# Polynomial convolution and self-attention on one core: the second image of the first pair in double chunks, and a new order in the first image's prologue

## The chip, the cores and the metric

One core of a Trainium2 chip runs the whole problem in one launch. The metric is the device time of that launch in microseconds; lower is better. Engines are named as in the profile: PE (matrix), PEld (its weight load), DVE (vector), ACT (scalar), POOL (GpSimd), SP (the queue that starts most transfers).

## The reference, cut to what matters

The input is 32 images of 64 channels and 56 x 56 pixels, in fp32. Layer 0 is a polynomial in each group of 8 channels, added to the input. Layer 1 is a non-local block whose attention matrix is normalised twice.

```python
# layer 0, per image, groups of 8 channels
p2 = x[:, :, I2] * x[:, :, J2]                  # all 36 pairs of a group
y2 = einsum(p2, W2) + b2
p3 = x[:, :, I3] * x[:, :, J3] * x[:, :, K3]    # all 120 triples
y3 = einsum(p3, W3) + b3
l  = inp + y2 * beta2 + y3 * beta3 * 0.1

# layer 1, per image, n = 56*56 = 3136 positions
g     = clip(bn1(conv1x1(l, w_inside)), 0, 6)
theta = l[:, :32]
f     = theta^T theta                           # 3136 x 3136
f     = softmax(f, over rows); f = softmax(f, over columns)
out   = f g / h * w
out   = bn2(depthwise3x3(out, w_dw)) + l
```

## The kernel before

Images go in 16 pairs, one image on each half of the 128 partitions. A pair is 49 attention tiles of 128 positions (24 for each image, and one that holds both remainders); `IT = 49`. For each tile `t` the loop issues `scores` in two halves (PE into PSUM, then DVE takes minima and copies out), `first_softmax` and `second_softmax` (two exponentials of 128 x 3136 on ACT), and, `LAG = 3` tiles later, `attend` (100 matmul records of PE into the `av` and `ax` banks). Between these, in gaps called `aux0` and `aux1`, stand *units* of other work: polynomial matmuls of an image to come (`poly`), or the 1x1 convolution (`g_in`). Both use the one PSUM region `ax`, so units follow each other: a unit fills it, `poly_out` or `g_out` takes it out on DVE, `prepare` sets it up again.

The polynomial of an image is worked in chunks of 242 columns (`PCH`, 13 chunks, the last of 232). For each chunk, SP loads rotated copies of the input ("0", "a", "2", "4", "b", and two of an unrotated copy, "c", held in `xc`); the generator `products` multiplies them on POOL: `q = x0*xa`, four rounds `q*x`, and one product of the two `xc`. `poly` multiplies each round by its weights. For later pairs all four 32-row groups `ks` of a pair are worked at once (`ALL`). In pair 0 the first image is made in a prologue, and the second (`TWO`, groups 2 and 3) during the first 14 tiles; then pair 1's 13 chunks (`ALL`) follow in the remaining tiles of pair 0.

Loads are limited by slots: `XB` gives 7 for "0" copies, 13 for other copies, 3 for `xc`; `ROOM` gives 8 for `q` and 20 for products. `plan` is the order of the loads, `prefetch` issues from it while slots and `credit` allow, `advance` issues products while `ROOM` allows. `held` and `taken` count at issue; the engines then wait on semaphores.

The prologue works the first image in 7 columns of 448 (`FCS`). `first_loads` issues 16 transfers, half on SP and half on ACT, into 28 parts of four tiles; `first_products` makes 11 products on DVE, `first_poly` multiplies them on PE, `first_out` adds the bias and the input, `first_g` makes the 1x1 convolution of the positions that are complete. Batch norm's constants need a square root on ACT. Theta of the first image is copied by `load_theta` through SP in two parts.

Every engine's instructions are kept in the order of the code (`Pinned`), by a helper whose line is 108. So all rows of the profile say L108, and tiles tell them apart.

```python
for c in range(1, NF):
    first_poly(c)
    first_out(c - 1)
    if c + 2 < NF:
        first_loads(c + 2)
    if c + 1 < NF:
        first_products(c + 1)
    if c == 5:
        load_theta(0, 0, FCS[5][0])
        for b in range(NPC):
            feed(0, b, TWO)
        credit[0] = 12
        advance()
    first_g(c - 1)
```

Of the kernel before, what the change touches and what calls it, by code (L numbers as in the profile page):

```python
# [35 lines left out]
PCH = -(-N // NPC)  # L36
PCS = [(p, min(PCH, N - p)) for p in range(0, N, PCH)]
NROT = 6
EXT = CPG + NROT - 1
# [30 lines left out]
def tile_poly_conv_attention(  # L70
# [136 lines left out]
    fx, fp = parts(firsts), parts(ys[1:] + [tt])  # L207
    fat = {"x": 0, "p": 0, "q": 0}
    fxs = {}
# [74 lines left out]

    s1 = rsqrt_eps("bn1", row("var1"), C)
    dve.tensor_tensor(s1, s1, row("gamma1"), ALU.mult)
    for j in range(2):
        dve.tensor_tensor(wit[:, j, :], wit[:, j, :], s1, ALU.mult)
    bias1 = const.tile([128, C], FP, name="bias1")
    dve.tensor_tensor(bias1, row("mean1"), s1, ALU.mult)  # L290
    dve.tensor_tensor(bias1, row("beta1"), bias1, ALU.subtract)
    bias1r = const.tile([128, GM, C], FP, name="bias1r")
    for k in range(GM):
        dve.tensor_copy(bias1r[:, k, :], bias1)


    s2 = rsqrt_eps("bn2", col("var2"), 1)
    dve.tensor_tensor(s2, s2, col("gamma2"), ALU.mult)
    dve.tensor_scalar(wdt, wdt, s2, W / H, ALU.mult, ALU.mult)
    bias2 = const.tile([128, 1], FP, name="bias2")  # L300
    dve.tensor_tensor(bias2, col("mean2"), s2, ALU.mult)
    dve.tensor_tensor(bias2, col("beta2"), bias2, ALU.subtract)

    prods = {}
# [9 lines left out]

    XB = {"x0": 7, "xs": 13, "xc": 3}
    held = dict.fromkeys(XB, 0)
# [4 lines left out]

    def start(out, in_):
        credit[0] -= 1
        sync.dma_start(out=out, in_=in_)

    def load_next():
        tag, key = plan.pop(0)  # L330
        n, c, ks, name, k = key
        p0, w = PCS[c]
        held[tag] += 1
        ident = f"{n}_{c}_{ks[0]}_{k}"
        if name == "c":
            t = xp.tile([128, 2, PCH], FP, name=f"xc_{ident}", tag=tag, bufs=XB[tag])
            at = slice(ks[0] * 32, ks[-1] * 32 + 32)
            for d in range(2):
                src = bass.AP(
                    x.tensor,  # L340
                    ((4 * n + ks[0]) * EXT + 4 * d) * 4 * N + p0,
                    [[EXT * 4 * N, len(ks)], [N, 32], [1, w]],
                )
                start(t[at, d, :w], src)
            loaded[key] = [t[at, d, :w] for d in range(2)]
            return
        t = xp.tile([128, PCH], FP, name=f"x{name}_{ident}", tag=tag, bufs=XB[tag])
        for s0, every, d, grow in LOADS[name]:
            src = bass.AP(
                x.tensor,  # L350
                ((4 * n + k) * EXT + d) * 4 * N + p0,
                [[N, 32], [grow * 4 * N, NSLOT // every], [1, w]],
            )
            start(t[s0::every, :w] if every > 1 else t[:, :w], src)
        loaded[key] = t[:, :w]

    def prefetch():
        while plan and held[plan[0][0]] < XB[plan[0][0]] and credit[0] >= 1:
            load_next()


    ROOM = {"q": 8, "pr": 20}
    taken = dict.fromkeys(ROOM, 0)

    def products(n, c, ks):

        p0, w = PCS[c]  # L370
        ident = f"{n}_{c}_{ks[0]}"

        def use(name, k=None):
            key = n, c, ks, name, k
            return loaded.pop(key)

        x0 = {}
        rounds = [{}]
        both = []
        prods[n, c, ks] = rounds, both  # L380
        yield "q", len(ks)
        for k in ks:
            yield "load", (n, c, ks, "a", k)
            x0[k] = use("0", k)
            xa = use("a", k)
            q = prp.tile([128, PCH], FP, name=f"q_{ident}_{k}", tag="q", bufs=ROOM["q"])[:, :w]
            pool.tensor_tensor(q, x0[k], xa, ALU.mult)
            rounds[0][k] = q
            held["xs"] -= 1
            prefetch()  # L390
        for r, of in enumerate(("0", "2", "4", "b")):
            rounds.append({})
            yield "pr", len(ks)
            for k in ks:
                if of != "0":
                    yield "load", (n, c, ks, of, k)
                xr = x0[k] if of == "0" else use(of, k)
                p = prp.tile([128, PCH], FP, name=f"p_{ident}_{k}_{r}", tag="pr", bufs=ROOM["pr"])[:, :w]
                pool.tensor_tensor(p, rounds[0][k], xr, ALU.mult)
                rounds[-1][k] = p  # L400
                held["x0" if of == "0" else "xs"] -= 1
                prefetch()
        at = slice(ks[0] * 32, ks[-1] * 32 + 32)
        yield "load", (n, c, ks, "c", None)
        yield "pr", 1
        both += use("c")
        p4 = prp.tile([128, PCH], FP, name=f"p4_{ident}", tag="pr", bufs=ROOM["pr"])[at, :w]
        pool.tensor_tensor(p4, both[0], both[1], ALU.mult)
        rounds.append({k: p4 for k in ks})
# [26 lines left out]
    def feed(n, c, ks):  # L436
        todo = [("x0" if name == "0" else "xs", name, k) for k in ks for name in "0a"]
        for name in "24bc":
            todo += [("xc", name, None)] if name == "c" else [("xs", name, k) for k in ks]
        for tag, name, k in todo:  # L440
            plan.append((tag, (n, c, ks, name, k)))
        feeds.append((products(n, c, ks), None))
# [11 lines left out]

    def poly(n, c, ks, rs):

        p0, w = PCS[c]
        rounds = prods[n, c, ks][0]
        at = slice(ks[0] * 32, ks[-1] * 32 + 32)
        for r in rs:  # L460
            for k in ks:
                pe.matmul(
                    out=ax[k * 32 : k * 32 + 32, AUX : AUX + w],
                    lhsT=wq[:, r, k % 2, :] if r < NRND else w4[at, k * 32 : k * 32 + 32],
                    rhs=rounds[r][k],
                    start=False,
                    stop=(r == NRND),
                    skip_group_check=True,
                )
            taken["pr" if r else "q"] -= 1 if r == NRND else len(ks)  # L470

    def poly_out(n, c, ks):

        p0, w = PCS[c]
        at = slice(ks[0] * 32, ks[-1] * 32 + 32)
        assert n < 3 or all((n - 3, b) in stored for b in range(NB))
        xc = prods.pop((n, c, ks))[1][0]
        held["xc"] -= 1
        dve.scalar_tensor_tensor(
            ys[n % 3][at, p0 : p0 + w], ax[at, AUX : AUX + w], bias0[at], xc, ALU.add, ALU.add  # L480
        )
# [3 lines left out]

    def load_theta(b, c0=0, c1=N):
        y = ys[b // 2 % 3]
# [3 lines left out]
        for r in range(4):  # L491
            start(ths[b][r * 32 : r * 32 + 32, c0:c1], y[p0 : p0 + CRED, c0:c1])

# [187 lines left out]
    def make_diags():  # L681

        eye = xp.tile([128, PCH], FP, name="eye", tag="xs", bufs=XB["xs"])[:, :128]
        pool.memset(eye, 0.0)
# [4 lines left out]
        for k in range(9):  # L689
            t = xp.tile([128, PCH], FP, name=f"diag_{k}", tag="xs", bufs=XB["xs"])[:, :128]  # L690
            pool.tensor_scalar(t, eye, wdt[:, k : k + 1], None, ALU.mult)
            diags.append(t)
# [47 lines left out]
    LAG = 3  # L740
    ALL, ONE, TWO = (0, 1, 2, 3), (0, 1), (2, 3)
    last = NP * IT
# [30 lines left out]

    def poly_unit(n, c, ks, rs, hs):
        ends = rs[-1] == NRND
        unit(
            hs,
            FOR_POLY,
            lambda: poly(n, c, ks, rs),
            (lambda: poly_out(n, c, ks)) if ends else None,  # L780
            1 + 3.6 * len(rs),
        )
        if ends and c == NPC - 1:
            for j in (0, 1):
# [38 lines left out]

    def first_g(c):
        for qs in GS:
            if min(len(FCS) - 1, ((qs[-1] + 1) * QT - 1) // FW) == c:
                g_in(0, qs, 0)
                g_out(0, qs, 0)
                prepare(FOR_G if qs[0] < NQ else FOR_POLY)

    prepare(FOR_G)
    NF = len(FCS)
    first_poly(0)
    for c in range(1, NF):
        first_poly(c)
        first_out(c - 1)
        if c + 2 < NF:
            first_loads(c + 2)
        if c + 1 < NF:
            first_products(c + 1)  # L840
        if c == 5:
            load_theta(0, 0, FCS[5][0])

            for b in range(NPC):
                feed(0, b, TWO)
            credit[0] = 12
            advance()
        first_g(c - 1)
    first_out(NF - 1)
    load_theta(0, FCS[5][0], N)  # L850
    first_g(NF - 1)


# [4 lines left out]
    for n in range(NP):  # L858
# [4 lines left out]
        def rounds(m, c, ks, per):  # L863
            return [("p", m, c, ks, list(range(r, r + per))) for r in range(0, NRND + 1, per)]

        todo = []
        if n == 0:
            for c in range(NPC):
                todo += rounds(0, c, TWO, 3)
# [196 lines left out]
```

## Time and profile before

| | |
|---|---|
| three runs | 4947.52, 4949.45 and 4963.6 us; median 4949.45 |
| the profiled execution | 4948.12 us, of which the span is 4946.3 us |
| granted PE clock, mean | 0.992 |
| first exponential (tile 0) starts | 97.09 us |
| stretch 97 to 218 us: PE busy | 105.13 of 121.00 us |
| stretch 218 to 503 us: PE busy | 256.25 of 285.00 us |
| stretch 503 to 797 us (one later pair): PE busy | 288.38 of 294.00 us |

A row of the time order gives start and duration in microseconds, engine, operation, output and inputs by the program's names, shape and count; in brackets stand the idle time of the engine before it and what ended that. A row of a table of stretches gives its length, the busy time of PE, PEld, DVE, ACT and POOL with the counts, the granted PE clock, and the share and rate of DMA. In rows of groups the busy time and the mean duration in ns are followed by the idle time before the group and its releasers. PE records each matmul of this kernel twice.

### The profile page before, as it was taken

The numbers are of one execution on the slowest core, as the hardware profiler recorded it, in microseconds if no ns is written. First come the engines' busy times: TensorE is split into PE (matmuls) and PEld (weight loads), VectorE is DVE, ScalarE is ACT, GpSimd is POOL, SyncE is SP. The second block draws the span as 40 slices with busy tenths as digits, with TensorE's granted clock in tenths as the row PEclk, the third lists the DMA queues.
The fourth block names the chain that finished last, engine by engine and source line by source line (L and its number), as shares of the span: only waits on it lengthen the run. The fifth ranks groups of instructions, "written<-read, shape, count | busy, mean of one in ns | idle before, by whom it ended". The sixth has DMA issues, their size and how long they took to land.

```text
span 4946.3 us, 264020 instructions
## 1 busy us (share of the span) xinstructions
PE 4734.2 (96%) x118122; PEld 3218.8 (65%) x118122; DVE 4125.5 (83%) x6100; ACT 4554.4 (92%) x2356; POOL 3222.6 (65%) x4335
## 2 busy tenths in 40 slices
PE   6898999999999999999999999999999999999887
PEld 2555666666666666666666666666666666666665
DVE  6545898888888898888889889898888889888887
ACT  1667999999999999999999999999999999999996
POOL 2677685858858586785857768585875858678000
PEclk8999999999999999999999999999999999999999
DMA  7555656565565655556555565656556565654201
GB/s 205 145 152 156 147 144 153 144 152 141 145 141 151 146 145 149 143 143 146 149 143 144 149 143 142 154 144 150 142 145 143 150 144 144 153 142 126 45 11 34
DMA packets 884318, 685.66 MB, mean 139 GB/s; under 512 B 290924, under 2 KB 869356, under 8 KB 879084
## 3 DMA queue, kind: packets, MB, share of 16 engines
q1 hardware_dynamic: 875180, 659.46, 52.5%
q8 instruction: 924, 15.14, 1.3%
q10 hardware_dynamic: 8000, 9.30, 0.6%
q14 instruction: 214, 1.75, 0.1%
HBM read 565.65 MB, written 25.69 MB: 120 GB/s over the span
## 4 chain that ended last, share of the span: by engine, by line
PE 77%; DVE 12%; DMA 3%; issue 3%; ACT 3%; POOL 1%; SPq 1%; ACTq 0%; DVEq 0%; POOLq 0%
PE av L108 33%; PE ps L108 26%; PE ax L108 18%; DVE e L108 10%; ACT e L108 3%; DMA xc_None<-in_x_dram 1%; POOL p L108 1%; DVE y L108 1%; DMA first<-in_x_dram 1%; DVE num L108 1%; DMA x<-in_x_dram 1%; SPq L108 1%; DMA xa<-in_x_dram 0%; DVE rd L108 0%; ACTq L108 0%
## 5 line engine op out<-in xcount | busy, mean ns | idle before, releaser
L108 PEld LDWEIGHTS av<-gq,e 128*64 128x64 f32 x64512 | 2012.2, 138 | 943.9 <-issue 936.2
L108 ACT ACTIVATE e<-e,nm 128x3136 f32<-128x3136 f32 x784 | 2283.6, 2913 | 279.9 <-DVE e L108 264.0
L108 POOL TENSOR_TENSOR p<-q,x 128x242 f32<-128x242 f32 (+1 forms) x2418 | 1824.3, 788 | 815.6 <-PE ax L108 801.2
L108 ACT ACTIVATE e<-e,rz 128x3136 f32<-128x3136 f32 x784 | 2270.3, 2896 | 0.0
L108 PE MATMUL av<-gq,e 128*64 128x65 f32 x64512 | 2225.5, 225 | 3.9 <-ACT e L108 3.1
L108 DVE TENSOR_SCALAR_CACHE_REDUCE e<-ps 128x1568 f32<-128x1568 f32 x784 | 1403.7, 1790 | 314.1 <-PE ps L108 294.2
L108 DVE TENSOR_SCALAR_CACHE_REDUCE e<-ps,nm 128x1568 f32<-128x1568 f32 x784 | 1448.6, 1848 | 255.7 <-PE ps L108 250.1
L108 PE MATMUL ps<-th 32*64 32x392 f32 x25088 | 1449.4, 515 | 120.7 <-DVE e L108 110.7
L108 POOL TENSOR_TENSOR q<-x,xa 128x242 f32<-128x242 f32 x806 | 574.2, 734 | 226.0 <-DMA xa<-in_x_dram 218.0
L108 DVE SCALAR_TENSOR_TENSOR y<-tt,wdt,y 128x605 f32<-128x605 f32 (+6 forms) x711 | 713.1, 1003 | 6.4 <-DMA tt<-tr 5.2
L108 POOL TENSOR_TENSOR p<-q,xb 128x242 f32<-128x242 f32 x806 | 573.9, 739 | 212.3 <-PE ax L108 204.5
L108 PEld LDWEIGHTS ps<-th 32*64 32x64 f32 x25088 | 369.8, 130 | 463.7 <-DVE e L108 381.5
L108 PE MATMUL ax<-gq,e 128*64 128x65 f32 x12288 | 489.7, 222 | 0.7 <-issue 0.6
L108 PE MATMUL ax<-p,wq 128*32 128x242 f32 (+1 forms) x6448 | 481.9, 374 | 1.8 <-POOL p L108 0.2
L108 PEld LDWEIGHTS ax<-gq,e 128*64 128x64 f32 x12288 | 425.0, 138 | 1.0 <-issue 1.0
L108 PEld LDWEIGHTS ax<-p,wq 128*32 128x32 f32 x6448 | 178.4, 109 | 111.8 <-POOL p L108 19.1
L108 POOL TENSOR_SCALAR y<-y,bias 128x616 f32<-128x616 f32 (+2 forms) x79 | 146.9, 1860 | 98.9 <-PE ax L108 98.9
L108 POOL TENSOR_TENSOR p<-xc_None 128x242 f32<-128x242 f32 (+3 forms) x208 | 127.6, 614 | 109.5 <-DMA xc_None<-in_x_dram 91.0
L108 DVE SCALAR_TENSOR_TENSOR y<-ax,bias,xc_None 128x242 f32<-128x242 f32 (+3 forms) x208 | 97.1, 467 | 116.8 <-PE ax L108 116.8
L108 PE MATMUL ax<-wit,y 128*64 128x64 f32 x3136 | 144.2, 223 | 11.7 <-issue 7.5
L108 PE MATMUL ax<-p,w 128*32 128x242 f32 (+1 forms) x1612 | 123.9, 370 | 32.1 <-POOL p L108 32.1
L108 ACT ACTIVATION_READ_ACCUMULATOR e<-e,nm 128x1 f32 x784 | 145.5, 186 | 0.0
(86 smaller groups left out, 1389.4 us busy)
## 6 DMA issues: line engine op xcount, KB each, us to landing
x<-in_x_dram SPq DMA_DIRECT2D x2232, 121.0 KB
xa<-in_x_dram SPq DMA_DIRECT2D x744, 121.0 KB
xb<-in_x_dram SPq DMA_DIRECT2D x1488, 60.5 KB
th<-y SPq DMA_DIRECT2D x124, 392.0 KB
xc_None<-in_x_dram SPq DMA_DIRECT2D x360, 121.0 KB
x<-in_x_dram SPq DMA_DIRECT2D x186, 116.0 KB
out_dram<-y SPq DMA_DIRECT2D x60, 308.0 KB
tt<-tr SPq DMA_DIRECT2D x128, 100.0 KB
```

The source lines that it names most:

```text
L108: i = f(*args, **kw)
```

## The change

In pair 0 the second image is worked in double chunks of 484 columns: one load, and one POOL product, covers two chunks, and PE multiplies the two halves one after the other, in the units and the order of before. The two `xc` copies still come by single chunks. Slots become parts of one ring tile for each kind, and a double takes two neighbouring ones. `XB` goes from 7, 13 and 3 to 6, 14 and 3.

In the prologue, a column's way out and the first G matmuls of the column before it go ahead of its polynomial on PE; what remains of G follows one column later. Batch norm's constants move into the loop, behind `first_loads(3)`. The feed of the second image starts at column 4 rather than 5, and both parts of theta are copied through ACT.

```diff
+DCS = [(p, min(2 * PCH, N - p)) for p in range(0, N, 2 * PCH)]
...
-    s1 = rsqrt_eps("bn1", row("var1"), C)
...
-    XB = {"x0": 7, "xs": 13, "xc": 3}
+    XB = {"x0": 6, "xs": 14, "xc": 3}
...
+    ring = {t: [xp.tile([128, m, PCH], FP, name=f"ring_{t}", tag=t, bufs=1), 0] for t, m in XB.items() if t != "xc"}
+    ringc = xp.tile([128, 2 * XB["xc"] * PCH], FP, name="ring_xc", tag="xc", bufs=1)
+
+    def chunks(ks):
+        return DCS if len(ks) < len(ALL) else PCS
+
+    def many(w):
+        return -(-w // PCH)
+
+    def take_ring(tag, w):
+        t, at = ring[tag]
+        m, size = many(w), t.shape[1]
+        if at % m or at + m > size:
+            at = 0
+        ring[tag][1] = (at + m) % size
+        return t[:, at : at + m, :].rearrange("p m w -> p (m w)")[:, :w]
...
-            q = prp.tile([128, PCH], FP, name=f"q_{ident}_{k}", tag="q", bufs=ROOM["q"])[:, :w]
+            q = take_ring("q", w)
             pool.tensor_tensor(q, x0[k], xa, ALU.mult)
...
-        p4 = prp.tile([128, PCH], FP, name=f"p4_{ident}", tag="pr", bufs=ROOM["pr"])[at, :w]
-        pool.tensor_tensor(p4, both[0], both[1], ALU.mult)
+        p4 = take_ring("pr", w)[at, :]
+        for sub in range(m):
+            yield "load", (n, c, ks, f"c{sub}", None)
+            both.append(use(f"c{sub}"))
+            pool.tensor_tensor(p4[:, sub * PCH : min((sub + 1) * PCH, w)], *both[sub], ALU.mult)
...
-            taken["pr" if r else "q"] -= 1 if r == NRND else len(ks)
+            if ends:
+                taken["pr" if r else "q"] -= (sub + 1) * (1 if r == NRND else len(ks))
...
+    def first_units(c):
+        return [qs for qs in GS if min(len(FCS) - 1, ((qs[-1] + 1) * QT - 1) // FW) == c]
+
+    def first_g(c, at=0):
+
+        for i, qs in enumerate(first_units(c)):
+            if at != 1 or i:
                 g_in(0, qs, 0)
+            if at is not None:
                 g_out(0, qs, 0)
                 prepare(FOR_G if qs[0] < NQ else FOR_POLY)
+            else:
+                return
...
     for c in range(1, NF):
-        first_poly(c)
         first_out(c - 1)
+        if c > 1:
+            first_g(c - 2, 1)
         if c + 2 < NF:
             first_loads(c + 2)
+        if c == 1:
+
+            s1 = rsqrt_eps("bn1", row("var1"), C)
...
+            prepare(FOR_G)
+        first_g(c - 1, None)
+        first_poly(c)
         if c + 1 < NF:
             first_products(c + 1)
+        if c == 4:
+
+            for b in range(len(DCS)):
+                feed(0, b, TWO)
+        if c >= 4:
+            credit[0] = 8
+            advance()
         if c == 5:
-            load_theta(0, 0, FCS[5][0])
-
-            for b in range(NPC):
-                feed(0, b, TWO)
-            credit[0] = 12
-            advance()
-        first_g(c - 1)
+            load_theta(0, 0, FCS[5][0], act)
     first_out(NF - 1)
-    load_theta(0, FCS[5][0], N)
+    load_theta(0, FCS[5][0], N, act)
+    first_g(NF - 2, 1)
     first_g(NF - 1)
```

## The prediction

> **What bounds the kernel now.** I read the page's engine and slice lines first, then stretches of the span, then the time order inside the two stretches that the change touches, then the chain and POOL's groups there.
>
> ```profile
> PE 4734.2 (96%) x118122; PEld 3218.8 (65%) x118122; DVE 4125.5 (83%) x6100; ACT 4554.4 (92%) x2356; POOL 3222.6 (65%) x4335
> 97.00:218.00 121.00, 105.13 (x1944) 60.03 (x1946) 62.09 (x98) 78.69 (x42) 91.15 (x138) 0.97 0.55 145
> 218.00:503.00 285.00, 256.25 (x5564) 160.05 (x5558) 157.26 (x248) 202.88 (x105) 197.13 (x297) 0.95 0.58 152
> 503.00:797.00 294.00, 288.38 (x7396) 198.91 (x7400) 256.88 (x376) 284.57 (x148) 211.90 (x278) 1.00 0.59 148
> ```
>
> The three stretches (PE, PEld, DVE, ACT, POOL busy, then clock and DMA) are: second image of pair 0 (97 to 218), all of pair 1's polynomial (218 to 503), and one later pair. A later pair takes 294 us with PE at 98%, and the same holds for every pair behind it. Pair 0 takes 406 us. In 97 to 218 PE is busy 105 of 121 us and nobody else is full: something is late.
>
> ```profile
> 116.78 2.91 ACT L108 ACTIVATE e<-e,nm 128x3136 f32<-128x3136 f32 x1 [0.88 <-DVE e L108]
> 217.75 2.91 ACT L108 ACTIVATE e<-e,nm 128x3136 f32<-128x3136 f32 x1 [3.98 <-DVE e L108]
> 161.83 0.60 PE L108 MATMUL ax<-q,wq 128*32 128x242 f32 x4
> 169.55 0.60 PE L108 MATMUL ax<-q,wq 128*32 128x242 f32 x4
> 181.60 1.01 PE L108 MATMUL ax<-p,wq 128*32 128x242 f32 x8
> 184.40 0.60 PE L108 MATMUL ax<-p,w 64*32 64x242 f32 x4 [1.79 <-POOL p L108]
> ...
> by line: DMA x<-in_x_dram 34.0%; POOL p L108 26.6%; SPq L108 17.3%; DMA xc_None<-in_x_dram 9.9%; issue 8.9%; DMA xb<-in_x_dram 7.0%; DVE e L108 4.0%; POOLq L108 0.2%
> 121.15 4.47 DMA xc_None<-in_x_dram
> ...
> L108 POOL TENSOR_TENSOR p<-q,x 128x242 f32<-128x242 f32 x67 | 44.8, 708 | 0.0
> L108 POOL TENSOR_TENSOR p<-xc_None 64x242 f32<-64x242 f32 x12 | 7.3, 612 | 28.8 <-DMA xc_None<-in_x_dram 25.3 <-PE ax L108 2.3 <-PE ps L108 1.2
> ```
>
> From tile 3 (116.78) to tile 14 (217.75) a tile takes 9.18 us. A tile in which PE waits for nobody takes 7.72 (161.83 to 169.55, same first unit a tile later); the usual one stalls before the last matmuls of a chunk (181.60 to 184.40). The chain of 120 to 165 is a loop of SP issues, transfers and POOL products, with no PE in it. POOL sits idle 28.8 us before the product of the two xc copies, because xc stands last in SP's order. SP gives 14 transfers per chunk at about 0.6 us each, 8.4 us plus waits for slots, and a chunk takes 9.3.
>
> The prologue is the other stretch:
>
> ```profile
> 34.02 1.28 ACT L108 ACT_TABLE_LOAD   x1 [34.02 <-DMA first<-in_x_dram]
> 35.61 0.55 DVE L108 RECIPROCAL r_bn<-s_bn 128x64 f32<-128x64 f32 x1 [4.88 <-ACT s_bn L108]
> 41.40 0.60 DVE L108 TENSOR_TENSOR tt<-first 128x448 f32<-128x448 f32 x1
> 79.97 0.61 DVE L108 TENSOR_TENSOR first<-first 64x448 f32<-64x448 f32 x1
> 87.47 1.61 PE L108 MATMUL ps<-th 32*64 32x392 f32 x16
> 91.04 4.10 PE L108 MATMUL ps<-th 32*64 32x392 f32 x16 [1.96 <-DVE e L108]
> 97.09 2.91 ACT L108 ACTIVATE e<-e,nm 128x3136 f32<-128x3136 f32 x1 [23.95 <-DVE e L108]
> ```
>
> DVE stands still until ACT has issued column 2's loads and can take the square root of the batch norm; products of column 2 start at 41.40, column 6's end at 80.58, the first exponential starts at 97.09, after a wait for theta's tail in the matmuls of 91.04.
>
> **The change part by part.**
>
> *Double chunks.* Per two chunks SP issues 16 transfers instead of 28 (xc stays in single chunks): 9.6 us. POOL does 10 products of 484 columns and two of xc. The trace has no 484-wide product. Upper bound twice the row, 2 x 708 = 1416 ns; below, 232 wide takes 682 to 688 and 242 wide 708, some 2.3 ns a column, so about 1250. The Trainium skill's "GPSIMD Engine Reference" (Performance versus the Vector engine) gives 2.6 cycles an element[...]. I take 1250, nearest to the trace. The sum is 10 x 1.25 + 2 x 0.61 = 13.7 us ([...]by the upper bound 15.4); PE needs two tiles, 15.4. So the verdict, PE bound, is the same with each.
>
> The slots decide whether it gets there. A double chunk takes 18 of the 20 pr slots, and they come free only as its second half is multiplied. With T the start of a chunk's third PE unit, POOL can do all but one product of the next chunk's first round from T+1.0: four products to T+6, three more (free since unit four, T+4.4) to T+9.8, then xc to T+11. PE wants the first three rounds at T+7.7 and xc's product at T+12.5. The margin is 1.5 us, 0.5 with the upper bound. The next chunk's q and first product end at T+14.8, before T+15.4.
>
> Here a rule speaks against the change: "DMA: Bandwidth & Descriptors" (Rules for kernel authors) says that a DMA whose outermost dimension has size c below 16 runs on at most c engines. The xc loads of this phase have 2 outermost, and stay so. The row agrees: 4.47 us to land for 60.5 KB, beside 3.13 for an x of 121 KB soon after. If the four in a row serialized into POOL's path as the two do now, the 28.8 us of idle would stay and the gain would be near nothing. I take the gain: the loads go out 10 us ahead of their product once SP is not full.
>
> Worth: tiles 3 to 14 take 11 x 7.72 less 1.35 for the one unit that its tile 8 lacks (0.43 + 0.92), 83.6 instead of 101.0: minus 17.4. The half clock at the end of the stretch (mean 0.97) may give 1 more; I leave 1.5 for small stalls. **Minus 17.**
>
> *Prologue order.* Removed: PE's first G matmuls behind a whole column of polynomial. Moved: batch norm behind first_loads(3). By the order of the changed program's instructions ACT now issues eight more loads before its square root, and every PE matmul of column 1 stands behind G of column 0, which needs batch norm. ACT's 8 loads took 6 us in before (38.75 to 44.80); now they start at 34.5, each behind the landing of the transfer eight places earlier, so the table load is near 42, and products of column 2 at 42 + 6.8 = 48.8 (6.8: 34.02 to 41.40 less the column's way out, now earlier). PE then starts column 1 after an idle stretch of 20 us. In before the clock is 0.50 from about 37 to 47 after an idle of 7; "TensorE: Matmul & The Clock Gate" (The HAM clock gate) says that an idle window of 3.4 us halves the clock until about as long of work: at full clock column 1 costs nothing beside DVE, at half clock its 4.8 us become about 7, and DVE's way out waits 2 us. By the row I take 2.
>
> Then DVE: 5.97 of products, 0.60 way out, 0.75 for G's way out and refill, 7.3 a column with no PE wait (before 7.1 to 9.3). End of products: 48.8 + 2 + 4 x 7.3 + 6 = 86.0 (was 80.58). Tail: way out, refill and first G 1.9; column 6's matmuls, now behind them, 4.8 (29.22 to 34.05); way out 0.7; three G rounds at 1.43, 4.3; two score halves with DVE 1.72 + 1.85 + 1.72 + 1.9. Together 18.8 (was 16.5). First exponential 104.8: **plus 8**, bounds plus 3 (ACT's loads at pure issue rate, warm clock) and plus 13.
>
> *Theta on ACT.* SP's queue loses 8 issues, theta's tail no longer stands behind 12 copies: minus 2.5, already in the tail above. But transfers take turns on eight semaphores, and theta's last one now follows a copy that waits for the ninth product of the first double chunk. POOL starts that near 85, the ninth ends at 96, its copy lands at 99, theta at 101.5, and the exponential follows 3 us later: 104.5, level with the other path, so not added. DMA queue order is what is queued behind it: SP's next copies, with time to spare.
>
> *Early feed.* Doubles go out from column 4: no cost ahead of the last first loads in SP's order; a chunk ready by 99, wanted at 106.
>
> *Rings, 6 and 14 slots.* From the first scores on, PE and DVE have the same instructions. In later pairs POOL waits 801 us for PE in one group of the page alone, which covers it; zero, bound plus 0.5 a pair either way.
>
> Sum against the profiled execution (4948.1 us; span 4946.3; 1.3 below the runs' median of 4949.45): 4948.1 - 17 + 8 = 4939.
>
> **The rivals.** (1) The prologue costs 0 to 2, as the matmuls of a column no longer tie DVE and loads(3) start 8 us earlier; against it stands DVE waiting on ACT; 4931. (2) The slots or the narrow xc loads stall each double chunk 2 us and more, or theta's semaphore adds 8: gain and loss cancel; for it the thin margin; 4950. (3) Slower: x0 falls from 7 to 6 slots in all pairs, SP stands before an x0 slot with theta, tt and out behind it, and PE waits at pair ends. Price: 15 pairs; from 1.6 us a pair (24 in all) it decides over my minus 9; at 1.8 a pair 4966. Against it: SP has some 370 transfers a pair (13 x 26, and theta, tt and out) at 0.64, about 235 of 294 us. (4) Doubles that do not arise: the instruction order shows them, so no chance.
>
> **How the numbers follow.** 0.3% (15 us) is about what a measurement can tell from no change. Likeliest 0.64, 4939; rival 1 0.17, 4931; rival 2 0.12, 4950; rival 3 0.07, 4966. Faster by over 0.3%, below 4933: most of rival 1 and a tenth of the likeliest, 0.21; slower, over 4963: rival 3 and a part of 2, 0.09; same 0.70. Range: plus 3 with minus 19, and rival 1, reach 4926; rival 2 reaches 4953.
>
> **What would show it.** After: tiles 3 to 14 at 7.7 to 7.9 us, POOL's wait for xc near nothing, 484-wide products near 1250 ns, table load near 42, first exponential near 105, the pair-1 stretch and later pairs unchanged. Wrong if tiles stay over 8.5, if the first exponential is before 99 or after 112, or if a later pair is off 294 by over 1.

## The result and the profile after

| | before | changed |
|---|---|---|
| median, 12 runs each (us) | 4951.25 | 4952.55 |
| span of the profiled execution (us) | 4946.3 | 4946.9 |
| first exponential starts (us) | 97.09 | 124.44 |
| mean tile from tile 3 to tile 14 (us) | 9.18 | 7.56 |
| first POOL product of pair 1 (us) | 213.7 | 217.1 |
| tile 48, the last of pair 0 (us) | 488.3 | 490.6 |

The ratio is 0.9997, 95% interval 0.9988 to 1.0005: no difference that can be measured. Two large changes cancel. The second image gained what was forecast, and the prologue lost more than three times what was forecast. (The kernel before was run again beside each experiment below, with medians from 4948.70 to 4948.96 us; ratios are to those runs.)

First the engines' line of the changed kernel's profile and its three stretches (PE, PEld, DVE, ACT, POOL busy, then clock, DMA share, GB/s):

```profile
PE 4722.0 (95%) x118122; PEld 3215.6 (65%) x118122; DVE 4120.5 (83%) x6100; ACT 4553.9 (92%) x2356; POOL 3208.4 (65%) x4275
97.00:218.00 121.00, 103.70 (x1812) 55.48 (x1810) 62.25 (x99) 73.75 (x39) 81.13 (x81) 0.89 0.54 151
218.00:503.00 285.00, 259.05 (x5696) 164.51 (x5696) 162.07 (x256) 209.11 (x109) 198.86 (x300) 0.94 0.58 151
503.00:797.00 294.00, 288.62 (x7394) 199.03 (x7378) 256.89 (x374) 281.57 (x147) 212.50 (x278) 1.00 0.58 146
```

The first stretch hides both changes: PE is busy for 103.70 us where it was 105.13, because 27 us of it are now prologue (its clock of 0.89 says so too), and the rest runs faster. The second stretch holds more PE work, 259.05 us against 256.25, which the prediction did not have. The later pair is as it was.

The second image, by tiles 3 and 14 in the time order, and then by POOL's groups between 97 and 218 us:

```profile
144.22 2.91 ACT L110 ACTIVATE e<-e,nm 128x3136 f32<-128x3136 f32 x1 [0.88 <-DVE e L110]
227.37 2.91 ACT L110 ACTIVATE e<-e,nm 128x3136 f32<-128x3136 f32 x1 [1.47 <-DVE e L110]
```

```profile
L110 POOL TENSOR_TENSOR ring_pr<-ring_q,ring_xs 128x484 f32<-128x484 f32 x36 | 42.6, 1227 | 0.0
L110 POOL TENSOR_TENSOR ring_pr<-ring_q,ring_x 128x484 f32<-128x484 f32 x10 | 12.2, 1223 | 29.5 <-PE ax L110 29.5
L110 POOL TENSOR_TENSOR ring_pr<-ring_xc 64x242 f32<-64x242 f32 x12 | 7.2, 616 | 6.8 <-DMA ring_xc<-in_x_dram 4.9 <-issue 1.5
```

Eleven tiles take 83.15 us instead of 100.97. A product of 484 columns takes 1227 ns. POOL waits 4.9 us for the xc copies; in the kernel before it was 27.4 in this stretch (total, number of waits, longest):

```profile
POOL p L108 <- DMA xc_None<-in_x_dram: 27.4, 11, 4.9
```

What POOL waits for now is PE, which has to free slots: 29.5 us, of which one wait of 18.6 is PE's late start.

The prologue, by the same rows that the prediction showed of before:

```profile
42.99 1.28 ACT L110 ACT_TABLE_LOAD   x1 [42.99 <-DMA first<-in_x_dram]
44.57 0.55 DVE L110 RECIPROCAL r_bn<-s_bn 128x64 f32<-128x64 f32 x1 [11.66 <-ACT s_bn L110]
49.78 0.61 DVE L110 TENSOR_TENSOR tt<-first 128x448 f32<-128x448 f32 x1
83.54 0.62 DVE L110 TENSOR_TENSOR tt<-first 128x448 f32<-128x448 f32 x1 [3.06 <-DMA first<-in_x_dram]
88.37 0.61 DVE L110 TENSOR_TENSOR first<-first 64x448 f32<-64x448 f32 x1
97.36 0.68 DVE L110 SCALAR_TENSOR_TENSOR y<-first,bias,first 64x448 f32<-64x448 f32 x1 [7.12 <-PE first L110]
101.86 2.86 PE L110 MATMUL ps<-th 32*64 32x392 f32 x12
109.89 1.57 PE L110 MATMUL ps<-th 32*64 32x392 f32 x4 [5.17 <-DMA th<-y]
120.93 1.57 PE L110 MATMUL ps<-th 32*64 32x392 f32 x4 [1.09 <-DMA th<-y]
124.44 2.91 ACT L110 ACTIVATE e<-e,nm 128x3136 f32<-128x3136 f32 x1 [5.46 <-DVE e L110]
```

Batch norm's wait grew from 4.88 to 11.66 us, as forecast. Scores begin at 101.86 (87.47 before), and then tile 0 takes 22.6 us to its exponential where it took 9.6. Of the time from 101.86 to 120.93, PE spends most in front of theta. The chain of waits of this stretch says what theta stood behind (start, duration, what):

```profile
94.20 4.79 POOL ring_pr L110 x5
...
100.00 1.18 POOL ring_pr L110
101.17 10.37 DMA ring_xs<-in_x_dram
...
111.61 5.47 DMA ring_xs<-in_x_dram
117.07 0.02 issue
117.09 3.79 DMA th<-y
120.88 0.04 issue
120.93 1.59 PE ps L110 x4
```

A POOL product, the eighth, frees the slot of a prefetch copy; that copy takes 10.37 us to land; the next copy on its completion semaphore (the counter that says that a transfer has landed) is issued at its landing; theta's last transfer is on that semaphore too, and is issued on ACT at 117.09, right behind the second landing.

### The profile page after: what moved, and what is told of

Same layout as the page of the kernel before. It is cut to its first block, busy times and chain, and to the rows that moved or that the text cites. A ratio compares the mean times of both kernels' runs of the same rounds, so it can differ in the third digit from the quotient of the medians.

```text
span 4946.9 us, 263995 instructions
## 1 busy us (share of the span) xinstructions
PE 4722.0 (95%) x118122; PEld 3215.6 (65%) x118122; DVE 4120.5 (83%) x6100; ACT 4553.9 (92%) x2356; POOL 3208.4 (65%) x4275
## 4 chain that ended last, share of the span: by engine, by line
PE 78%; DVE 11%; issue 3%; DMA 3%; ACT 3%; POOL 1%; SPq 1%; ACTq 0%; DVEq 0%; POOLq 0%
PE av L110 33%; PE ps L110 26%; PE ax L110 19%; DVE e L110 9%; ACT e L110 3%; DMA ring_xs<-in_x_dram 2%; POOL ring_pr L110 1%; DVE y L110 1%; DVE num L110 1%; SPq L110 1%; DMA ring_xc<-in_x_dram 1%; DMA first<-in_x_dram 1%; PE first_s L110 0%; DMA th<-y 0%; POOL ring_q L110 0%
## 5 line engine op out<-in xcount | busy, mean ns | idle before, releaser
L110 POOL TENSOR_TENSOR ring_pr<-ring_q,ring_xs 128x242 f32<-128x242 f32 (+2 forms) x2382 | 1784.5, 783 | 533.7 <-PE ax L110 522.8
L110 POOL TENSOR_TENSOR ring_pr<-ring_q,ring_x 128x242 f32<-128x242 f32 (+2 forms) x794 | 606.2, 789 | 607.4 <-PE ax L110 574.8
L110 POOL TENSOR_TENSOR ring_q<-ring_x,ring_xs 128x242 f32<-128x242 f32 (+2 forms) x794 | 570.3, 745 | 169.3 <-DMA ring_xs<-in_x_dram 166.4
L110 PE MATMUL ax<-ring_pr,wq 128*32 128x242 f32 (+1 forms) x6448 | 474.5, 373 | 2.2 <-POOL ring_pr L110 1.1
L110 PEld LDWEIGHTS ax<-ring_pr,wq 128*32 128x32 f32 x6448 | 177.0, 109 | 106.9 <-POOL ring_pr L110 13.3
L110 DVE SCALAR_TENSOR_TENSOR y<-ax,bias,ring_xc 128x242 f32<-128x242 f32 (+3 forms) x208 | 97.0, 467 | 102.6 <-PE ax L110 102.6
L110 POOL TENSOR_TENSOR ring_pr<-ring_xc 128x242 f32<-128x242 f32 (+3 forms) x208 | 127.7, 615 | 67.8 <-DMA ring_xc<-in_x_dram 59.2
L110 PEld LDWEIGHTS ax<-wit,y 128*64 128x64 f32 x3136 | 118.9, 139 | 37.0 <-issue 18.7
## 6 DMA issues: line engine op xcount, KB each, us to landing
ring_xs<-in_x_dram SPq DMA_DIRECT2D x1440, 60.5 KB
```

What stands on the lines that cost most here:

```text
L110: i = f(*args, **kw)
```

## The experiments

*Theory A*: theta on ACT takes its turn on the DMA semaphores between prefetch copies that wait for POOL, and this, not the doubles or the load on the engines, holds tile 0. *Rival*: the transfer engines are full, and theta is late in any order. *Theory B*: the gain of the second image comes from the double chunks. *Rival*: from the slots and rings, or from the lead that a late PE gives POOL. A third question came up on the way: why pair 1 ended only 2.3 us later than before when tile 15 was 8.7 us late.

**theta_sp: the changed kernel, theta on SP, and the prefetch around it held to 8 and then 4 issues.**

```diff
-        if c >= 4:
-            credit[0] = 8
-            advance()
+            credit[0] = 8
+            advance()
         if c == 5:
-            load_theta(0, 0, FCS[5][0], act)
+            load_theta(0, 0, FCS[5][0])
+            credit[0] = 4
+            advance()
     first_out(NF - 1)
-    load_theta(0, FCS[5][0], N, act)
+    load_theta(0, FCS[5][0], N)
```

The first two added lines stand under `if c == 4:`.

> The changed kernel with theta's eight transfers on SP: head ahead of the third round's copies, tail behind the last column's way out and ahead of the xc copies. Main theory: what held tile 0 from 101.9 to 120.9 us was theta on ACT, each transfer behind a prefetch copy on the same DMA semaphore. Then theta's tail lands near 102, the first exponential is at 109 (101.9 plus the 7.3 us of four score groups with DVE between them) instead of 124.4, tiles 3 to 13 stay at 7.72, and the time falls by about 15 us, to 4937. Rival: the transfers are slow because the engines are full with prefetch copies in any order; then theta lands after 108, the first exponential is at 115 to 119, and the time falls by 5 to 9.

Measured: 4935.09 us, ratio to before 0.9976 (0.9967 to 0.9985). The first exponential is at 111.87; the scores start at 103.77, two microseconds late because the table load was (45.11), and take 8.1 us to the exponential. In the time order:

```profile
93.36 4.24 SPq L110 DMA_DIRECT2D th<-y  x4
101.61 3.66 SPq L110 DMA_DIRECT2D th<-y  x4
103.77 2.59 PE L110 MATMUL ps<-th 32*64 32x392 f32 x16
105.31 2.38 SPq L110 DMA_DIRECT2D ring_xc<-in_x_dram  x4
111.87 2.91 ACT L110 ACTIVATE e<-e,nm 128x3136 f32<-128x3136 f32 x1 [23.29 <-DVE e L110]
```

Theta's last transfer is issued by 105 and lands at 107.5, later than the 102 expected and near the rival's 108, yet PE hardly waits for it now (0.7 us at its weight loads). 12.6 us of the late start are gone, and 17 us of the time by the medians (10 by the two ratios to before). The edit moves the prefetch copies too, so the next run changes the queue alone.

**old_theta_act: the converse, one edit.** The double chunks behind the old prologue (old_prologue, below), and theta on ACT.

```diff
-            load_theta(0, 0, FCS[5][0])
+            load_theta(0, 0, FCS[5][0], act)
...
-    load_theta(0, FCS[5][0], N)
+    load_theta(0, FCS[5][0], N, act)
```

> As old_prologue, with one edit: theta's eight transfers on ACT instead of SP. In program order they then take the semaphores that they have in the changed kernel, the last one behind the copy that waits for POOL's ninth double product. Main theory: this alone brings the late start. POOL's products begin 4.7 us earlier here than in the changed kernel (84.9 against 89.6), where theta's last transfer landed at 120.9; so it lands near 116, the first exponential is near 119 to 120 instead of 96.5, and the time rises from 4925.7 to 4945 to 4950. Rival: theta was late only because the changed kernel's prologue gave the copies out too early and too many; then the first exponential is at 97 to 104 and the time stays under 4933.

Measured: 4941.31 us, ratio to before 0.9976 (0.9964 to 0.9988), against 4925.66 for old_prologue. The first exponential is at 114.49 instead of 96.53, 18 us later, where 23 were expected and the rival had at most 7: theta landed at 110.9. Its chain of waits has the same links as the changed kernel's, a copy of 9.22 us and one of 5.23 on theta's semaphore:

```profile
91.73 0.91 POOL ring_pr L110
92.65 9.22 DMA ring_xs<-in_x_dram
...
101.94 5.23 DMA ring_xs<-in_x_dram
107.17 0.02 issue
107.19 3.74 DMA th<-y
110.93 0.04 issue
110.97 1.59 PE ps L110 x4
```

So the choice of queue for eight transfers costs, by itself, 18 us at the first exponential, and 16 us of the whole time by the medians (9 by the ratios, whose intervals overlap a little). In the instructions of all these runs the transfers of SP and ACT share eight completion semaphores, and each waits for the landing of the one before it on its own. On SP, theta's place among the copies is fixed by SP's order; on ACT it is fixed by nothing but the turn that it was given.

**bn_back: theta_sp, and batch norm where it was.**

```diff
     first_loads(2)
+    s1 = rsqrt_eps("bn1", row("var1"), C)
...
-        if c == 1:
-            s1 = rsqrt_eps("bn1", row("var1"), C)
...
```

> As theta_sp, and the batch norm back ahead of the loop (before column 3's loads on ACT). Main theory: table load near 34 instead of 43, DVE's wait for the square root near 5 instead of 11.7, column 2's products start near 42, and all of it reaches the end of the prologue: first exponential near 101, time about 4929. Rival: column 6's loads, 3 us late in the changed kernel, become the bound and give half of it back: 105, 4933.

Measured: 4925.86 us, ratio 0.9956 (0.9941 to 0.9971). The first exponential is at 102.27, 9.6 us earlier than in theta_sp:

```profile
33.31 1.28 ACT L110 ACT_TABLE_LOAD   x1 [33.31 <-DMA first<-in_x_dram]
34.90 0.55 DVE L110 RECIPROCAL r_bn<-s_bn 128x64 f32<-128x64 f32 x1 [4.20 <-ACT s_bn L110]
```

The main theory holds, with the first exponential 1.3 us behind its 101 and the time 3 us under its 4929; column 6's loads were late by 3.0 us here as in the changed kernel, and cost nothing more.

**old_prologue: doubles and rings, all of the old prologue.** Theta on SP, batch norm ahead of the loop, the old order of a column, feed at column 5.

```diff
-        first_out(c - 1)
-        if c > 1:
-            first_g(c - 2, 1)
...
-        first_g(c - 1, None)
         first_poly(c)
+        first_out(c - 1)
...
+        first_g(c - 1)
...
```

> Double chunks, rings and slots of the changed kernel, with the prologue of the kernel before in its order, theta on SP. Main theory: first exponential at 97 to 100, tiles 3 to 13 at 7.72, so tile 15 is 16 to 19 us earlier than in the kernel before; pair 1's stretch is a chain of loads and products whose end moves with its start, which takes another 6; time about 4927. Rival: the second image was only fast because the late start gave POOL a lead of 27 us; then tiles 3 to 13 average over 8.2 and the time is 4936 or more.

Measured: 4925.66 us, ratio 0.9957 (0.9942 to 0.9971); first exponential at 96.53, tiles 3 to 14 at 7.56 us, tile 15 19.0 us earlier than before, tile 48 25.3 us. Each number is within 1.5 us of the main theory's. With POOL 11.7 us ahead of the first exponential, as in the kernel before (11.8), and not 34.8 as in the changed one, the doubles are as fast. Against bn_back it starts 5.7 us earlier and ends level. Taken out one after the other, theta's queue, batch norm's place and the rest of the new prologue give back 12.6, 9.6 and 5.7 us at the first exponential.

**single: the changed kernel, single chunks.**

```diff
-DCS = [(p, min(2 * PCH, N - p)) for p in range(0, N, 2 * PCH)]
+DCS = PCS
```

> The changed kernel with single chunks for the second image too (rings, slots 6 and 14 and the new prologue stay). Main theory: the double chunks alone bring the gain of the second image, so tiles 3 to 13 are back near 9.2 us; the copies ahead of theta's tail are half as large and wait for fewer products, so the first exponential is at 112 to 120; the end of pair 1 comes later by as much as the first image's second half does; time about 4966. Rival: the new slot counts or the rings bring the gain; then tiles 3 to 13 stay near 7.7 and the time is near 4945.

Measured: 4960.57 us, ratio 1.0019 (1.0009 to 1.0029). Slower, as the main theory had it, but tiles 3 to 14 are at 7.80 us, which is the rival's number and not the 9.2 of the main theory. The first exponential is at 121.28, and POOL had begun at 88.0: 33 us of lead instead of 12. So either the slots or the lead makes up for the single chunks.

**single_old: the same edit on old_prologue.**

> The prologue of the kernel before and single chunks, only the rings and the slot counts 6 and 14 of the change left. Main theory: rings and slots do nothing, so tiles 3 to 13 are back at 9.2 us, POOL's products for the second image take 125 to 130 us (127.7 in the kernel before), pair 1's begin near 213, and the time is that of the kernel before within 4 us. Rival: the slots, not the doubles, shortened the second image; then tiles 3 to 13 are at 7.8 and the time is near 4930.

Measured: 4948.09 us, ratio 0.9997 (0.9988 to 1.0006); tiles 3 to 14 at 9.10 us, POOL's second image 128.4 us long. Rings and slots do nothing that can be measured. In single it was the lead: the same slow chain, started 33 us ahead of PE, is only caught up at the end, where tile 13 takes 9.73 us.

That answers theory B and leads to the third question. From the time order of POOL, in nine kernels:

| kernel | POOL, second image: first to last product | POOL, pair 1 | tile 15, against before | pair 1's first product, against before | tile 48, against before |
|---|---|---|---|---|---|
| before | 85.3 to 213.0 | 213.7 to 462.7 | 0 | 0 | 0 |
| changed | 89.6 to 216.4 | 217.1 to 464.0 | +8.7 | +3.4 | +2.3 |
| single | 88.0 to 222.7 | 223.4 to 472.7 | +9.8 | +9.7 | +10.0 |
| single_old | 84.9 to 213.4 | 214.0 to 464.4 | +0.4 | +0.4 | +3.0 |
| theta_sp | 91.8 to 203.7 | 204.4 to 453.0 | -4.0 | -9.3 | -9.7 |
| old_theta_act | 82.6 to 206.1 | 206.8 to 453.7 | -1.5 | -6.9 | -8.1 |
| bn_back | 80.9 to 194.2 | 194.8 to 440.1 | -13.5 | -18.8 | -22.6 |
| xc_early | 87.1 to 195.0 | 195.7 to 444.5 | -12.7 | -18.0 | -19.4 |
| old_prologue | 84.9 to 188.7 | 189.3 to 437.4 | -19.0 | -24.3 | -25.3 |

Pair 1's products take 245 to 250 us in each kernel, and tile 48 follows the start of the last one by 24 to 27 us. The changed kernel and single reach tile 15 within 1.1 us of each other and end pair 0 7.7 us apart; POOL's starts on pair 1 are 6.3 apart.

The two marks are not free of each other. With double chunks the first product of pair 1 stands 16.4 us ahead of tile 15, in all seven such kernels (early_bn, below, is the seventh); with single chunks 11.1 us, in all three. At the end of the second image POOL is ahead of PE with doubles, and stands before slots that PE has to free; with single chunks it is late, and PE waits for it. The changed kernel, then two rows of the kernel before, the second from its waits between 150 and 236 us:

```profile
213.06 3.25 POOL L110 TENSOR_TENSOR ring_pr<-ring_q,ring_xs 128x232 f32<-128x232 f32 x5 [2.51 <-PE ax L110]
```

```profile
213.00 0.59 POOL L108 TENSOR_TENSOR p<-xc_None 64x232 f32<-64x232 f32 x1 [2.01 <-DMA xc_None<-in_x_dram]
PE ax L108 <- POOL p L108: 9.5, 6, 2.1
```

So the doubles bring 5.3 us that tile 15 does not show; a chain 2.1 us shorter (247.0 against 249.0) and 1.0 us more behind it make up the 6.4. What a change of the first 230 us is worth is therefore read at POOL's first product of pair 1 rather than at PE's tile, and to some 3 us only: bn_back starts pair 1 5.5 us behind old_prologue and ends level with it. No run moves POOL's start without tile 15, so that the end follows this start, and not what moves both, is argued and not shown.

**xc_early: what holds that chain of 248 us.** old_prologue with the xc copies given out ahead of the b copies.

```diff
-        for name in "24bc":
+        for name in "24cb":
```

> As old_prologue, with the xc copies of every chunk given out ahead of its b copies instead of behind them. In pair 1 POOL waits 23.6 us for xc copies between 215 and 437 us. Main theory: pair 1's stretch is bound by SP's issues (28 to a chunk at 0.64 us are 17.9 of the 19 us that a chunk takes), so POOL then waits for b copies instead and the time moves by less than 3 us from old_prologue's 4925.7. Rival: the late, narrow xc copies are a link of the chain; then their 23.6 us go, pair 1's products end 12 to 24 us earlier, and the time is 4902 to 4914.

Measured: 4932.11 us, ratio 0.9961 (0.9946 to 0.9976). In pair 1 the main theory holds: the chain is 248.8 us long (248.1 in old_prologue), and POOL's waits for copies between 215 and 437 us only changed their names (the lines for copies add up to 36.3 and 41.8 us). POOL's one long wait in this stretch, which most of the traces put down to PE, is 9 us with single chunks and 18 to 19 with doubles, and does not change the length either. First old_prologue's, then xc_early's:

```profile
POOL ring_pr L110 <- DMA ring_xc<-in_x_dram: 23.6, 8, 3.9
POOL ring_q L110 <- DMA ring_xs<-in_x_dram: 8.9, 13, 2.4
```

```profile
POOL ring_q L110 <- DMA ring_xs<-in_x_dram: 29.6, 31, 2.4
POOL ring_pr L110 <- DMA ring_xs<-in_x_dram: 12.2, 15, 2.0
```

So the wait for xc is not what sets the length. That SP's issues set it is the theory's reading: SP itself waits 49 us for POOL in that stretch of old_prologue, a loop of slots between the two fits as well, and no run takes issues away.

But the median rose by 6.4 us, which neither theory had. The ratios alone (0.9961 and 0.9957) would not tell the two apart; the profiles do, with tile 48 5.9 us later. It is in the prologue: the first exponential is at 102.81, 6.3 late. The four narrow xc copies of the first double now stand in front of theta's tail, land 5.4 to 8.1 us after their issue, and theta behind them takes 6.4 to 7.9; the chain of waits shows one of them:

```profile
91.13 0.40 SPq L110
91.53 0.04 issue
91.58 6.95 DMA th<-y
98.53 0.04 issue
98.57 2.32 PE ps L110 x12
```

In old_prologue, ahead of the xc copies, the same transfers landed in 3.0 to 3.9 us.

**early_bn: a version from these results.** old_prologue, with the two square roots ahead of column 1's loads on ACT, and batch norm's small arithmetic on POOL.

```diff
     first_loads(0)
+    root1, root2 = root("bn1", row("var1"), C), root("bn2", col("var2"), 1)
     first_loads(1)
...
-    s1 = rsqrt_eps("bn1", row("var1"), C)
-    dve.tensor_tensor(s1, s1, row("gamma1"), ALU.mult)
+    s1 = rsqrt_eps(*root1)
+    pool.tensor_tensor(s1, s1, row("gamma1"), ALU.mult)
...
```

> As old_prologue, with batch norm's square roots ahead of column 1's loads on ACT and its small arithmetic on POOL, which has nothing to do then, so that DVE neither waits 4.3 us for the square root nor spends 5 us on the small operations. Main theory: DVE sets the pace of the prologue, the first exponential comes 7 to 9 us earlier than 96.5, POOL's products and pair 1 move with it, time about 4918. Rival: the transfers set the pace (the engines' share is 0.83 to 0.91 from 15 to 70 us); then the first exponential is at 94 to 96 and the time 4923 to 4926.

Measured: 4920.22 us, ratio to before 0.9935 (0.992 to 0.9949), the lowest median of all, though its interval overlaps old_prologue's. But the rival was right on the prologue: the first exponential is at 95.54, only 1.0 earlier than in old_prologue. DVE's waits from 15 to 97 us show why, first old_prologue's, then early_bn's:

```profile
DVE r_bn L110 <- ACT s_bn L110: 4.6, 2, 4.3
DVE y L110 <- DMA first<-in_x_dram: 4.0, 3, 2.1
```

```profile
DVE y L110 <- DMA first<-in_x_dram: 12.1, 5, 4.5
```

The wait for the square root is gone, and that for column loads took its place: they became the limit. (The engines' share that the rival rests on holds but for 30 to 40 us, where it is 0.48 in old_prologue: the very stretch of the square root.) Where the rest of its 5.4 us came from is not settled. Pair 1's first product is 0.7 us earlier, its chain 1.5 us shorter, and the distance between the two grows on from 2.2 us at tile 48 to 7.3 at tile 400 and 5.7 at the last one; a part may lie between executions.

## Why the prediction was right and wrong

*The sum* was 4939 for a gain of 17 and a loss of 8. The changed kernel is level with the kernel before: the doubles gained 18.6 us up to tile 15 and 6.4 behind it, the prologue lost 27.4, and 1.7 came in the later pairs, less than what separates two executions. "Same" was the likeliest verdict, and it held; that the time lies in the range, half a microsecond from its top, is luck: two terms were wrong by 19 and 8 us, with opposite signs. The place is that of rival 2, whose "theta's semaphore adds 8" names the right link, though its other half, doubles that stall, did not happen. And one of the prediction's own signs of being wrong came true: a first exponential after 112.

*Double chunks: right in the second image.* 11 tiles gained 17.8 us (17.4 in the sum before the 1.5 kept back); the product of 484 columns took 1227 ns beside my 1250. The Trainium skill's "GPSIMD Engine Reference" (Performance versus the Vector engine) puts such a product at 2.6 cycles an element, an estimate of 2.17 ns a column at the 1.2 GHz of its example; from the 708 ns of 242 columns to the 1227 of 484 it is 2.14, where I had read 2.3. The slots held: from 150 to 236 us PE waited for no product. old_prologue and single_old show that doubles do this alone.

*The narrow xc loads: right where I weighed them, wrong where I did not.* POOL's wait for them fell from 27.4 to 4.9 us. The Trainium skill's "DMA: Bandwidth & Descriptors" (Rules for kernel authors) confines such a copy to at most as many engines as its outermost dimension has; I asked only what that costs POOL. What it costs is behind it in the queues: 6.3 us when theta stood there (xc_early). In the changed kernel the xc copies took 4.6 to 10.7 us to land, and the ring_xs copy behind them 10.37.

*Prologue order: the sizes that failed.* Working down the steps:

| step | predicted | measured |
|---|---|---|
| products of column 2 start | +7.4 | +8.4 (41.40 to 49.78) |
| from there to the end of products, against 39.2 before | -2.0 | 0.0 (49.78 to 88.98) |
| end of products to first scores, 6.9 before | +4.7 | +6.0 |
| first scores to first exponential, 9.6 before | -2.4 | +13.0 |
| sum | +7.7 | +27.4 |

The moved batch norm was sized well, and bn_back returned 9.6 for it. The saving in the columns did not come: they ran at 7.13 us each where 7.3 was computed, but column 6's loads were 3.06 us late, which the sum did not have. The tail's extra came as forecast but for PE's half clock in a part of column 6's matmuls, which the sum had charged to column 1 only: DVE waited 7.12 us, and the clock over 90 to 100 us was 0.83.

*Theta on ACT: the step that failed.* I named the mechanism and then called it level, "so not added". Three terms of that chain were short. POOL began at 89.6, not 85. The ninth product was over at 102.4, not 96; the chain hangs on the eighth, over at 101.2. And I let one copy follow it, of 3 us, where the chain has two in a row on one semaphore, 10.37 and 5.47 us; that is 12.8 of the 19.4 us by which theta was late. Theta landed at 120.9, not 101.5. theta_sp and old_theta_act show the cause from both sides.

*"The pair-1 stretch unchanged": wrong, and in the kernel's favour.* I carried PE's shift through to the end, as if the stretch began with PE's tile 15. It begins with POOL's first product, and the doubles move that 5.3 us further than tile 15. 6.4 us of the loss at tile 15 were gone by tile 48, most of it that way, and the doubles' whole worth is 25 us (25.3 in old_prologue), not 17.

*Later pairs and x0's six slots: right.* single_old, with slots and rings alone, is at 0.9997.

## What to carry to other kernels

Before moving a transfer to another queue, write down which landing each of its issues will wait for: here completion semaphores are shared between two queues, and a short, urgent transfer inherits the wait of the prefetch in front of it. Put urgent transfers ahead of prefetches in one queue's own order, and narrow ones last. And when several chained engines are late, find the mark with which the length of the next phase stays the same, and count the gain there: here it was POOL's first product of pair 1, and a sum taken at PE's tile 15 was 6.4 us off.

## What the runs showed of the hardware that was not expected

A transfer's time to land grew threefold with what was in front of it. In the changed kernel the double copies (484 columns, 242 KB) landed in 2.9 us at the head of the queue, in up to 7.1 us in the crowd that followed, and in 8.8 to 10.4 us right behind the four xc copies of 60.5 KB and 64 partitions; in old_prologue, behind the same four, in 7.4. The mean DMA share from 100 to 110 us was 0.75 and 0.57.

The traces also bear on why the narrow copies are slow. A transfer's completion semaphore is updated 16 times for every other kind of transfer in these kernels, the 64-partition b copies among them, but 3 times for an xc copy of pair 0, whose outermost dimension is 2, and 5 times for one of the later pairs, whose outermost dimension is 4. That fits two and four engines; no run here shows the engines one by one.
